# Joining triangular inverses: two heads per pass instead of one

## The chip, the cores and the metric

The kernel runs on one core of a Trainium2 chip. The time is device microseconds of one execution, the median of three runs. A core has TensorE (matrix products, written to PSUM), VectorE, ScalarE and GpSimd (work on tiles in SBUF and PSUM) and SyncE, which here only issues transfers. Each engine works off its own instructions in order; semaphores tie them together. Tiles lie over up to 128 partitions; a tile in PSUM takes a bank of its own here, and the kernel's pools hold eight of them. TensorE's array of 128 by 128 can be used in part: a product whose operands lie in partitions 32 to 63 uses one *row group*, and the partitions of its output pick the *column group*. Two products on different groups can be in the array together. All numbers here are float32, and each matrix product appears as two MATMUL instructions in the trace, each with its weight load.

## The reference

One block of a transformer: a gated delta-rule attention over 8 sequences of 256 tokens, with 16 key heads of width 128 and two value heads for each, and then a sparse feed-forward layer. What matters here is the recurrence:

```python
def step(S, inp):
    q_t, k_t, v_t, b_t, d_t = inp
    Sk = jnp.einsum('bhi,bhipj->bhpj', k_t, S)
    dv = b_t[..., None] * (v_t - Sk)
    upd = jnp.einsum('bhi,bhpj->bhipj', k_t, dv)
    S = S * d_t[:, :, None, :, None] + upd
    o = jnp.einsum('bhi,bhipj->bhpj', q_t, S)
    return (S, o)
...
x = x + ga * _L0_attn_ref(h, ...)
...
x = x + gb * _L0_ffn_ref(h, ...)
return x
```

The kernel does not step through the tokens. It cuts each sequence into two chunks of 128 tokens and solves a chunk at once: that takes the inverse T of a 128 by 128 triangular matrix (ones on the diagonal, and in the triangle the products of keys, weighted by decay and beta), for each sequence, chunk and value head.

## The kernel before

The work goes by *groups*: two sequences (`bp`) and four key heads (`GH = 4`), 16 groups in all. A *head* below is one key head for two sequences; it has 2 sequences x 2 chunks x 2 value heads = 8 triangular matrices (`NP = 8`, of which `NS = 4` belong to each sequence). There are 64 heads.

For each group, ahead of its use:

- `stage_a` (L479) makes the keys of a head (ps_k L432, then the convolution), their products ps_kk (L532) and the 8 triangles a_t (L563). It writes the four 32 by 32 diagonal blocks of each triangle to scr in DRAM.
- `stage_b` (L577) loads the blocks of all four heads (128 of them, one per partition) and inverts them by substitution on VectorE (L604, L610). It writes the inverses twice, to scr_y as they are and to scr_x transposed.

For each head then:

- `levels` (L674) joins the diagonal inverses to the full T in t_inv. For two neighbouring diagonal blocks with inverses X and Y, and the block A of the triangle between them, the block of T is -X A Y. It is done twice: 32-wide (blocks 0 with 1 and 2 with 3, both for 8 triangles), then 64-wide (upper with lower half). Each level is two bursts of matmuls with copies between them: ps_w L703 (A by X), copied to w1 (L711, L712); ps_t L717 (by Y), negated into t_inv (L729, L738), and, transposed on VectorE (L725, to `low`), into x_top (L732); ps_w2 L743/L746, copied to w2 (L750); ps_t2 L754/L757, negated into t_inv (L760, L761). In the trace ps_w2 and ps_t2 stand under the names ps_w and ps_t, as numbers are left out.
- In the 32-wide bursts the matmuls use two squares of the array in turn (`h` in 0, 1): rows 0 to 31 to columns 32 to 63, and rows 64 to 95 to columns 96 to 127 in ps_w, the other way round in ps_t. In the 64-wide bursts the first four triangles go from the upper 64 rows to the lower 64 columns, and the last four, whose operands are moved to the other half through low_up and x_top, from the lower rows to the upper columns.
- `prepare` (L619) makes queries, values and the gate of the next head (ps_qv L432, ps_z L646). `attend` (L764) uses T for one sequence of the head (ps_v L779, ps_kq L791 to L795, ps_u L810, ps_ks L818, ps_o L837 and L859, ps_u L853), `shares` projects two heads' outputs (ps_y L907).
- `feed_forward` (L160) of finished sequences and `ahead` (the next group's stage_a and stage_b) are pushed along a step at a time by `along` (L1089).

The loop over heads (L1102) is a round robin of generators: each turn asks attend of both sequences of this head, levels of the next head, and prepare of the next head for one step. Each head's levels thus run during the head before, the first head's of a group during the last head of the group before, after `all_of(background)` has finished stage_b (L1131). t_inv has two buffers, one in use by attend, one being made. The scheduler turns this trace into an order for each engine beforehand; the order of one engine does not change at run time.

Two more things matter. PSUM is shared by pools: ps_inv (L86, two banks) holds the bursts of levels, ps_kk, ps_ff (L183) and ps_out (L238); ps_in and ps_mix (three banks each) hold the rest. And SyncE issues all transfers of levels: two to x_even (L687), four to t_inv (L690), four to x_top (L693), and two to low_up (L697, L730) per head.

## Time and profile before

| what | value |
|---|---|
| median of three runs | 2133.49 us (2126.72 to 2134.71) |
| span of the profiled execution | 2126.1 us |
| mean granted TensorE clock | 0.988 |
| PE busy | 2054.1 us (97%) |
| DVE busy | 1660.8 us (78%) |
| ACT busy | 1356.1 us (64%) |
| POOL busy | 367.8 us (17%) |
| matmuls of levels: L703, L717 (32-wide) | 2048 instructions each, median 191 ns |
| matmuls of levels: L743, L746, L754, L757 (64-wide) | 512 instructions each, median 218 ns |
| copies of levels on ACT: L711, L712, L729, L738, L750, L760, L761 | 64 of each, 363 to 380 ns |
| the same, L732 | 128, 308 ns |
| transposes of levels on DVE: L725 | 64, median 430 ns |
| transfers of levels on SyncE, from issue to landing | 1.9 to 2.5 us (medians by line) |

The profile is one execution, and its time is its span (from the first to the last instruction). PE is TensorE, PEld its weight loads, DVE VectorE, ACT ScalarE, POOL GpSimd, SP SyncE. Matmuls overlap each other, so the duration of one is longer than the time from its start to the next start, and a busy TensorE is not one at its peak. In a line of the groups, "out<-in" names the tiles, then come the shapes and the count, the busy time and the mean of one, and the idle time just before with what ended it. In the timeline, a row is a run of like instructions: its start, how long it took, and the count.

### The profile page before, as it was taken

What the parts mean: (1) busy time and instruction counts of PE and PEld (TensorE: products, weight loads), DVE (VectorE), ACT (ScalarE), POOL (GpSimd) and SP (SyncE); (2) the same over time, 40 slices, a digit from 0 to 9 for tenths busy, and PEclk for the clock granted to TensorE, in tenths of its full rate; (3) what the DMA queues carried; (4) which work ended last, traced back from release to release, by engine and by line L of the source; (5) the groups of instructions that cost most, each with busy time, mean ns of one, the idle gap of its engine ahead of it and who ended that gap; (6) DMA issues with size and microseconds to landing.
All of it is one profiled execution on the core that took longest, in us unless ns stands there. A gap on an engine that the chain in (4) does not pass through costs nothing.

```text
span 2126.1 us, 46444 instructions
## 1 busy us (share of the span) xinstructions
PE 2054.1 (97%) x16684; PEld 1633.6 (77%) x16684; DVE 1660.8 (78%) x4039; ACT 1356.1 (64%) x4579; POOL 367.8 (17%) x375
## 2 busy tenths in 40 slices
PE   8989999999999999999999999999999999999998
PEld 5567777777777787778778687778778778787887
DVE  6788787878879587897878779787896958879357
ACT  3577767776766467576576666667666656666552
POOL 3121202112120111212021020211112011120010
PEclk9999999999999999999999999999999999999999
DMA  4342424233242443434343343443434244343236
GB/s 135 98 112 69 113 66 118 79 78 113 82 116 82 124 118 92 124 97 120 115 103 102 117 117 104 113 118 98 121 98 120 67 124 129 96 114 96 73 90 216
DMA packets 324517, 226.85 MB, mean 107 GB/s; under 512 B 254520, under 2 KB 266168, under 8 KB 324288
## 3 DMA queue, kind: packets, MB, share of 16 engines
q1 hardware_dynamic: 304416, 163.34, 28.8%
q10 hardware_dynamic: 19872, 60.54, 9.1%
q8 instruction: 133, 2.18, 0.4%
q14 instruction: 96, 0.79, 0.1%
HBM read 186.28 MB, written 29.12 MB: 101 GB/s over the span
## 4 chain that ended last, share of the span: by engine, by line
PE 66%; DVE 13%; DMA 7%; ACT 6%; issue 2%; SPq 1%; POOL 1%; ACTq 0%; DVEq 0%; POOLq 0%
PE ps_qv L432 10%; PE ps_y L907 9%; PE ps_z L646 8%; PE ps_ks L818 5%; PE ps_ff L190 4%; PE ps_k L432 3%; DVE cv L420 3%; PE ps_u L853 2%; PE ps_out L244 2%; PE ps_o L837 2%; PE ps_kk L532 2%; PE ps_gt L893 2%; PE ps_o L859 2%; DMA blk<-scr 2%; PE ps_u L810 2%
## 5 line engine op out<-in xcount | busy, mean ns | idle before, releaser
L420 DVE SCALAR_TENSOR_TENSOR cv<-ps_qv,conv_sb,cv 128x510 f32<-128x510 f32 (+1 forms) x564 | 410.0, 736 | 43.4 <-ACT cv L418 41.5
L432 PE MATMUL ps_qv<-h_bp,wh 128*128 128x512 f32 x768 | 367.3, 602 | 3.0 <-DVE cv L420 2.0
L105 POOL TENSOR_TENSOR rs<-ss,minus_halves 128x4 f32<-128x4 f32 x128 | 133.2, 1049 | 1040.8 <-DVE ss L864 1023.7
L646 PE MATMUL ps_z<-wh,h_bp 128*128 128x256 f32 x1024 | 249.9, 386 | 12.1 <-ACT gz L653 11.3
L907 PE MATMUL ps_y<-wo,og_p 128*128 128x256 f32 x1024 | 236.0, 380 | 0.9 <-DVE cv L420 0.9
L646 PEld LDWEIGHTS ps_z<-wh,h_bp 128*128 128x128 f32 x1024 | 186.3, 192 | 39.8 <-ACT gz L653 12.4
L432 PEld LDWEIGHTS ps_qv<-h_bp,wh 128*128 128x128 f32 x768 | 133.3, 192 | 105.4 <-issue 97.8
L418 ACT ACTIVATE cv<-ps_qv,conv_sb 128x512 f32<-128x512 f32 x188 | 129.3, 690 | 122.3 <-PE ps_qv L432 121.9
L907 PEld LDWEIGHTS ps_y<-wo,og_p 128*128 128x128 f32 x1024 | 188.0, 190 | 23.7 <-DVE cv L420 1.4
L604 DVE TENSOR_TENSOR tmp<-blk 128x30 f32<-128x30 f32 (+14 forms) x480 | 157.1, 327 | 46.8 <-DMA blk<-scr 37.6
L516 POOL TENSOR_TENSOR diag<-consts,bk 128x1032 f32<-128x1032 f32 x64 | 122.8, 1918 | 371.6 <-DVE bk L507 371.6
L844 ACT ACTIVATE junk<-o 128x128 f32<-128x128 f32 x512 | 154.1, 305 | 42.9 <-DVE o L860 36.4
L551 DVE TENSOR_TENSOR_SCAN e<-dbc,diag 128x1032 f32<-128x1032 f32 x60 | 137.9, 2299 | 47.6 <-POOL diag L516 46.3
L610 DVE TENSOR_TENSOR blk<-blk,tmp 128x30 f32<-128x30 f32 (+14 forms) x480 | 156.9, 327 | 9.6
L420 DVE SCALAR_TENSOR_TENSOR k_t<-ps_k,conv_sb,k_t 128x510 f32<-128x510 f32 (+1 forms) x189 | 139.2, 738 | 22.0 <-ACT k_t L418 20.3
L877 DVE SCALAR_TENSOR_TENSOR og<-o,rs,gz 128x128 f32<-128x128 f32 x512 | 143.9, 345 | 14.1 <-POOL rs L105 14.0
L818 PE MATMUL ps_ks<-u,cross 128*128 128x128 f32 x1024 | 144.7, 284 | 2.8 <-DVE aq L800 1.5
L784 ACT ACTIVATE vn<-ps_v,nk 128x256 f32<-128x256 f32 x256 | 105.7, 482 | 62.0 <-PE ps_v L779 61.2
L818 PEld LDWEIGHTS ps_ks<-u,cross 128*128 128x128 f32 x1024 | 133.7, 197 | 12.5 <-ACT u L812 5.3
L190 PE MATMUL ps_ff<-h,w_ff 128*128 128x128 f32 x1024 | 130.5, 277 | 3.3 <-ACT h L149 2.3
L190 PEld LDWEIGHTS ps_ff<-h,w_ff 128*128 128x128 f32 x1024 | 123.5, 192 | 10.8 <-issue 3.8
L432 PE MATMUL ps_k<-h_bp,wk 128*128 128x512 f32 x256 | 123.9, 609 | 2.0 <-ACT junk L451 1.2
(176 smaller groups left out, 4259.2 us busy)
## 6 DMA issues: line engine op xcount, KB each, us to landing
wh<-in_w_heads ACTq DMA_DIRECT2D x64, 640.0 KB, 4.1
w_ff<-in_w_ff SPq DMA_DIRECT2D x128, 256.0 KB, 3.0
dbc<-d_dram SPq DMA_DIRECT2D x60, 516.0 KB, 4.2
wo<-in_w_heads ACTq DMA_DIRECT2D x32, 512.0 KB, 3.7
w_dn<-in_w_down SPq DMA_DIRECT2D x64, 256.0 KB, 3.4
wk<-in_w_keys SPq DMA_DIRECT2D x16, 512.0 KB, 5.0
scr<-a_t SPq DMA_DIRECT2D x256, 32.0 KB, 2.4
blk<-scr SPq DMA_DIRECT2D x16, 512.0 KB, 3.7
```

Of the source, the lines that this page charges most:

```text
L105: nc.gpsimd.tensor_tensor(out=out, in0=in_, in1=minus_halves[:, :n], op=ALU.pow)
L190: nc.tensor.matmul(ps[:, a, l, :], lhsT=w[:, k, l, :], rhs=h2[:, k, :], start=(k == 0), stop=(k == CC - 1),)
L420: nc.vector.scalar_tensor_tensor(out=dst[:, :, d:], in0=ps[:, :, : T - d], scalar=taps[:, KC - 1 - d : KC - d], in1=dst[:, :, d:], op0=ALU ...
L432: nc.tensor.matmul(ps.rearrange("p b t -> p (b t)"), lhsT=w[k], rhs=h_bp[:, k, :], start=(k == 0), stop=(k == CC - 1),)
L551: nc.vector.tensor_tensor_scan(e.rearrange("p i s t -> p (i s t)"), dbc.rearrange("p i f -> p (i f)"), diag.rearrange("p s t -> p (s t)"), ...
L604: nc.vector.tensor_tensor(out=tmp, in0=blk[:, j, None, j + 1 :].to_broadcast([P, j, m]), in1=blk[:, 0:j, j, None].to_broadcast([P, j, m]), ...
L610: solved = nc.vector.tensor_tensor(out=blk[:, 0:j, j + 1 :], in0=blk[:, 0:j, j + 1 :], in1=tmp, op=ALU.subtract)
L646: nc.tensor.matmul(ps[:, n, :], lhsT=h_bp[:, k, i * T + n * P : i * T + (n + 1) * P], rhs=wh[:, k * 640 + 384 : (k + 1) * 640], start=(k = ...
L818: nc.tensor.matmul(ps_ks[:, ct, h, :], lhsT=cross[:, h, ct, :], rhs=u0[:, h, :], start=True, stop=True)
L844: nc.scalar.activation(junk, o[:, n, h, :], AF.Square, accum_out=ss[:, n, h : h + 1])
L877: nc.vector.scalar_tensor_tensor(out=og[:, n, h, :], in0=o[:, n, h, :], scalar=rs[:, 2 * n + h : 2 * n + h + 1], in1=gz[:, i, n, h, :], op ...
L907: nc.tensor.matmul(ps_y[:, n, :], lhsT=og_p[:, j // 2, i, n, j % 2, :], rhs=wo[:, j // 2, j % 2, :], start=(j == 0), stop=(j == 3),)
```

## The change

`levels` takes two heads at a time (`pair`, two records, and two t_inv buffers `tts`).

- The 32-wide bursts hold the matmuls of both heads: the first head's go from the even 32-row groups to the odd column groups in ps_w, the second head's from the odd row groups to the even column groups, and the other way round in ps_t. A new tile `moved` holds the second head's blocks on the partitions that this needs. All four write one PSUM bank, 64 instructions to a burst.
- One copy negates all of ps_w into w1; ps_t is copied unnegated in four pieces, and VectorE transposes its two lower pieces straight into x_top, so `low` goes.
- The 64-wide bursts hold the matmuls of both heads on all four 64 by 64 squares: the squares that write the same partitions write different banks, so each burst has two PSUM tiles (`i` = 0 for the first four triangles of a head, 1 for the last four), 32 instructions to a burst. w2 is copied with negation in two pieces, the result in four pieces without.
- Tiles grow: t_inv has three buffers instead of two, x_top, low_up and w2 double. The program is built with `dynamic_dma_scratch_size=1024`.
- The loop calls levels for heads 0 and 1 before the loop begins and for the next two heads in every second head (`hp` odd).

```diff
@@ -409,8 +409,8 @@
         modulation(0)
-        t_inv = [single.tile([P, 2 * NS, P], F32, name=f"t_inv{i}") for i in range(2)]
-        x_top = single.tile([P, NS, 2 * Q], F32, name="x_top")
+        t_inv = [single.tile([P, 2 * NS, P], F32, name=f"t_inv{i}") for i in range(3)]
+        x_top = single.tile([P, 2 * NS, 2 * Q], F32, name="x_top")
         for t in (*t_inv, x_top):
             nc.gpsimd.memset(t, 0.0)
@@ -671,94 +671,103 @@
                 step()
                 yield
-        def levels(rec, scr_x, scr_y, tt):
-            hp = rec["hp"]
+        def levels(pair, scr_x, scr_y, tts):
+            hp = pair[0]["hp"]
             xv = scr_x.rearrange("(g s q) a b -> g q a s b", g=GH, q=NQ)
             yv = scr_y.rearrange("(g s q) a b -> g q a s b", g=GH, q=NQ)
-            a_f = rec["a"].rearrange("p i s t -> p (i s) t")
+            a_f = [rec["a"].rearrange("p i s t -> p (i s) t") for rec in pair]
             NP = 2 * NS
+            def rows(q, n=1):
+                return slice(q * Q, (q + n) * Q)
             x_even = single.tile([P, NP, Q], F32, name="x_even")
-            low_up = single.tile([P, NS, 2 * Q], F32, name="low_up")
-            for q in (0, 2):
-                nc.sync.dma_start(out=x_even[q * Q : (q + 1) * Q], in_=xv[hp, q])
-            for q in (1, 3, 0, 2):
-                rows = slice(q * Q, (q + 1) * Q)
-                nc.sync.dma_start(out=tt[rows, :, rows], in_=yv[hp, q])
-                if q < 2:
-                    for i in range(2):
-                        nc.sync.dma_start(
-                            out=x_top[i * 2 * Q + q * Q : i * 2 * Q + (q + 1) * Q, :, rows],
-                            in_=xv[hp, q, :, i * NS : (i + 1) * NS],
-                        )
-            nc.sync.dma_start(out=low_up[2 * Q :], in_=a_f[0 : 2 * Q, NS:, 2 * Q :])
-            even = [slice(0, Q), slice(2 * Q, 3 * Q)]
-            odd = [slice(Q, 2 * Q), slice(3 * Q, P)]
+            moved = single.tile([P, NP, Q], F32, name="moved")
+            low_up = single.tile([P, NP, 2 * Q], F32, name="low_up")
+            for r in range(2):
+                for h in range(2):
+                    nc.sync.dma_start(out=x_even[rows(2 * h + r)], in_=xv[hp + r, 2 * h])
+            for h in range(2):
+                nc.sync.dma_start(out=moved[rows(2 * h + 1)], in_=a_f[1][rows(2 * h), :, rows(2 * h + 1)])
+            for q in (1, 3):
+                nc.sync.dma_start(out=tts[0][rows(q), :, rows(q)], in_=yv[hp, q])
+                nc.sync.dma_start(out=moved[rows(q - 1)], in_=yv[hp + 1, q])
+            for r in range(2):
+                for q in range(2):
+                    nc.sync.dma_start(out=x_top[rows(2 * r + q), :, rows(q)], in_=xv[hp + r, q])
+            for r, q in ((0, 2), (1, 2), (1, 3), (0, 0), (1, 0), (1, 1)):
+                nc.sync.dma_start(out=tts[r][rows(q), :, rows(q)], in_=yv[hp + r, q])
+            nc.sync.dma_start(out=low_up[rows(2, 2)], in_=a_f[1][rows(0, 2), :, rows(2, 2)])
             ps = bank(ps_inv, [P, NP, Q], "ps_w")
             for s in range(NP):
                 for h in range(2):
+                    even, odd = rows(2 * h), rows(2 * h + 1)
                     nc.tensor.matmul(
-                        ps[odd[h], s, :],
-                        lhsT=a_f[even[h], s, odd[h]],
-                        rhs=x_even[even[h], s, :],
-                        start=True,
-                        stop=True,
+                        ps[odd, s, :], lhsT=a_f[0][even, s, odd], rhs=x_even[even, s, :], start=True, stop=True
+                    )
+                    nc.tensor.matmul(
+                        ps[even, s, :], lhsT=moved[odd, s, :], rhs=x_even[odd, s, :], start=True, stop=True
                     )
             w1 = single.tile([P, NP, Q], F32, name="w1")
-            nc.scalar.copy(w1[odd[0]], ps[odd[0]])
-            nc.scalar.copy(w1[odd[1]], ps[odd[1]])
+            nc.scalar.activation(w1, ps, AF.Copy, scale=-1.0)
             yield
             ps = bank(ps_inv, [P, NP, Q], "ps_t")
             for s in range(NP):
                 for h in range(2):
+                    even, odd = rows(2 * h), rows(2 * h + 1)
                     nc.tensor.matmul(
-                        ps[even[h], s, :],
-                        lhsT=w1[odd[h], s, :],
-                        rhs=tt[odd[h], s, odd[h]],
-                        start=True,
-                        stop=True,
+                        ps[even, s, :], lhsT=w1[odd, s, :], rhs=tts[0][odd, s, odd], start=True, stop=True
                     )
-            low = mixp.tile([Q, NP, Q], F32, tag="low", name="low", bufs=1)
-            nc.vector.transpose(
-                low.rearrange("p s t -> p (s t)"),
-                ps[even[0]].rearrange("p s t -> p (s t)"),
-            )
-            nc.scalar.activation(tt[even[1], :, odd[1]], ps[even[1]], AF.Copy, scale=-1.0)
-            nc.sync.dma_start(out=low_up[0 : 2 * Q], in_=tt[2 * Q :, NS:, 2 * Q :])
+                    nc.tensor.matmul(
+                        ps[odd, s, :], lhsT=w1[even, s, :], rhs=moved[even, s, :], start=True, stop=True
+                    )
+            for r in range(2):
+                nc.scalar.copy(tts[r][rows(2), :, rows(3)], ps[rows(2 + r)])
             for i in range(2):
-                nc.scalar.activation(
-                    x_top[i * 2 * Q + Q : (i + 1) * 2 * Q, :, 0:Q],
-                    low[:, i * NS : (i + 1) * NS],
-                    AF.Copy,
-                    scale=-1.0,
-                )
-            nc.scalar.activation(tt[even[0], :, odd[0]], ps[even[0]], AF.Copy, scale=-1.0)
-            yield
-            top, bottom = slice(0, 2 * Q), slice(2 * Q, P)
-            ps = bank(ps_inv, [P, NS, 2 * Q], "ps_w2")
+                part = slice(i * NS, (i + 1) * NS)
+                nc.sync.dma_start(out=low_up[rows(0, 2), part], in_=tts[1 - i][rows(2, 2), part, rows(2, 2)])
+            for r in range(2):
+                nc.vector.transpose(x_top[rows(2 * r + 1), :, rows(0)], ps[rows(r)])
+            for r in range(2):
+                nc.scalar.copy(tts[r][rows(0), :, rows(1)], ps[rows(r)])
+            yield
+            halves_of = rows(0, 2), rows(2, 2)
+            top, bottom = halves_of
+            first, second = slice(0, NS), slice(NS, NP)
+            lhs = a_f[0][top, :, bottom], low_up[bottom]
+            ps = [bank(ps_inv, [P, NS, 2 * Q], f"ps_w2{i}") for i in range(2)]
             for s in range(NS):
-                nc.tensor.matmul(
-                    ps[bottom, s, :], lhsT=a_f[top, s, bottom], rhs=x_top[top, s, :], start=True, stop=True
-                )
-                nc.tensor.matmul(
-                    ps[top, s, :], lhsT=low_up[bottom, s, :], rhs=x_top[bottom, s, :], start=True, stop=True
-                )
-            w2 = single.tile([P, NS, 2 * Q], F32, name="w2")
-            nc.scalar.copy(w2, ps)
-            yield
-            ps = bank(ps_inv, [P, NS, 2 * Q], "ps_t2")
+                for i in range(2):
+                    for r in range(2):
+                        nc.tensor.matmul(
+                            ps[i][halves_of[r if i else 1 - r], s, :],
+                            lhsT=lhs[r][:, i * NS + s, :],
+                            rhs=x_top[halves_of[r], i * NS + s, :],
+                            start=True,
+                            stop=True,
+                        )
+            w2 = single.tile([P, NP, 2 * Q], F32, name="w2")
+            for i, part in enumerate((first, second)):
+                nc.scalar.activation(w2[:, part], ps[i], AF.Copy, scale=-1.0)
+            yield
+            ps = [bank(ps_inv, [P, NS, 2 * Q], f"ps_t2{i}") for i in range(2)]
             for s in range(NS):
-                nc.tensor.matmul(
-                    ps[top, s, :], lhsT=w2[bottom, s, :], rhs=tt[bottom, s, bottom], start=True, stop=True
-                )
-                nc.tensor.matmul(
-                    ps[bottom, s, :], lhsT=w2[top, s, :], rhs=low_up[top, s, :], start=True, stop=True
-                )
-            nc.scalar.activation(tt[top, 0:NS, bottom], ps[top], AF.Copy, scale=-1.0)
-            nc.scalar.activation(tt[top, NS:, bottom], ps[bottom], AF.Copy, scale=-1.0)
+                for i in range(2):
+                    for r in range(2):
+                        side = halves_of[r if i else 1 - r]
+                        p = i * NS + s
+                        nc.tensor.matmul(
+                            ps[i][halves_of[r], s, :],
+                            lhsT=w2[side, p, :],
+                            rhs=tts[r][bottom, p, bottom] if r == i else low_up[top, p, :],
+                            start=True,
+                            stop=True,
+                        )
+            for i, part in enumerate((first, second)):
+                for r in range(2):
+                    nc.scalar.copy(tts[r][top, part, bottom], ps[i][halves_of[r]])
             yield
         def attend(rec, i, cv, gz, eps_q, tt, og_t):
@@ -1075,7 +1084,6 @@
         waiting = iter(())
         units = []
         head = 0
-        solved = False
         for g, (bp, k0) in enumerate(groups):
             ya = y_of[bp % 2]
             next_recs, next_scratch = [], []
@@ -1106,8 +1114,8 @@
                     gen, shared = prepared[head]
                     with tc.issue_after(first_solved):
                         all_of(gen)
-                if not solved:
-                    for _ in levels(rec, *scratch, t_inv[head % 2]):
+                if head == 0:
+                    for _ in levels(recs[:2], *scratch, [t_inv[r] for r in range(2)]):
                         along()
                 turns, ends[:] = ends[:], []
                 if hp % 2 == 0:
@@ -1122,19 +1130,19 @@
                             ),
                         )
                     waiting = shares(ya, k0 + hp == 0, og_p, wo, 6)
-                turns += [attend(rec, i, *shared, t_inv[head % 2], og_p[:, hp % 2, i]) for i in range(2)]
-                solved, coming = False, None
+                turns += [attend(rec, i, *shared, t_inv[head % 3], og_p[:, hp % 2, i]) for i in range(2)]
+                coming = None
                 if hp + 1 < GH:
-                    coming = recs[hp + 1], scratch
+                    coming = recs[hp + 1 : hp + 3], scratch
                 elif g + 1 < len(groups):
                     all_of(background)
-                    coming = next_recs[0], next_scratch
+                    coming = next_recs[:2], next_scratch
                 if coming:
-                    solved = True
-                    turns.append(levels(coming[0], *coming[1], t_inv[(head + 1) % 2]))
+                    if hp % 2 == 1:
+                        turns.append(levels(coming[0], *coming[1], [t_inv[(head + r) % 3] for r in (1, 2)]))
                     if head > 0:
-                        to_come = coming[0]
+                        to_come = coming[0][0]
                         gen, shared = begin(to_come["kh"], to_come["bp"], to_come["h"])
                         turns.append(gen)
                 while turns:
@@ -1207,7 +1215,7 @@
         "w_down": w_down,
         "table": table,
     }
-    nc = bacc.Bacc("TRN2", target_bir_lowering=False, num_devices=1)
+    nc = bacc.Bacc("TRN2", target_bir_lowering=False, num_devices=1, dynamic_dma_scratch_size=1024)
     sent, args = {}, {}
     for name, a in arrays.items():
         a = np.ascontiguousarray(a)
```

## The prediction

> **What bounds the kernel now.** I read the page first, then the groups of instructions with shapes kept apart, then TensorE's timeline in one head (1012 to 1037 us) and across one change of group (1058 to 1092 us), then the waits by line.
>
> ```profile
> span 2126.1 us, 46444 instructions
> PE 2054.1 (97%) x16684; PEld 1633.6 (77%) x16684; DVE 1660.8 (78%) x4039; ACT 1356.1 (64%) x4579; POOL 367.8 (17%) x375
> ...
> PE   8989999999999999999999999999999999999998
> ...
> L703 PE MATMUL ps_w<-x_even,a_t 32*32 32x32 f32 x2048 | 53.7, 194 | 7.0 <-DMA x_even<-scr_x 6.9
> ...
> L743 PE MATMUL ps_w<-x_top,a_t 64*64 64x64 f32 x512 | 45.4, 230 | 3.8 <-ACT x_top L732 2.5 <-DMA out<-res 1.3
> ...
> 1013.00 0.69 PE L703 MATMUL ps_w<-x_even,a_t 32*32 32x32 f32 x32
> 1013.62 1.13 PE L432 MATMUL ps_qv<-h_bp,wh 128*128 128x512 f32 x2
> ...
> 1031.14 0.22 PE L743 MATMUL ps_w<-x_top,a_t 64*64 64x64 f32 x1
> 1031.14 0.22 PE L746 MATMUL ps_w<-x_top,low_up 64*64 64x64 f32 x1
> 1031.20 0.22 PE L743 MATMUL ps_w<-x_top,a_t 64*64 64x64 f32 x1
> 1031.20 0.22 PE L746 MATMUL ps_w<-x_top,low_up 64*64 64x64 f32 x1
> 1031.26 0.22 PE L743 MATMUL ps_w<-x_top,a_t 64*64 64x64 f32 x1
> ...
> 1047.56 1.88 PE L432 MATMUL ps_qv<-h_bp,wh 128*128 128x512 f32 x4
> 1049.28 0.59 PE L791 MATMUL ps_kq<-cv,k_t 128*128 128x256 f32 x2
> ...
> 47.96 1.85 PE L399 MATMUL ps_m<-sc_t,wmod_ss 128*128 128x8 f32 x16
> 49.73 0.60 PE L1049 MATMUL ps_gate<-wmod_gates,sc_t 128*8 128x512 f32 x1
> ...
> PEld ps_w L703 <- DMA x_even<-scr_x: 8.8, 10, 2.4
> ```
>
> TensorE is busy in every slice, but busy hides pipelining, so I go by starts. Four 512-column matmuls start 1.72 us before what follows (1047.56 to 1049.28): 430 ns each, where the "mean of one" says 602. Pricing every matmul by the spacing of its shape (512 columns 430 ns, 256 columns 216, 128 columns 111, and the joins below) gives 1908 us of work in the 2126.1. The other 200 us, **9.4%**, is waiting, some 30 of it the ends of the small bursts. So TensorE's issue sets the end nine tenths of the time; VectorE (78%) and ScalarE (64%) follow it. What shortens TensorE's queue shortens the span.
>
> The joins (L703, L717, L743/L746, L754/L757) run once per head, 64 times. A 32-wide burst has 32 instructions (16 matmuls, two instructions each) and holds the queue 0.62 us (1013.00 to 1013.62). Single starts inside it alternate 7 ns and 25 ns: the two row groups start almost together, and a step of two takes 32 ns. Entry and exit add 21 and 96 ns. In a 64-wide burst the pair again starts within 7 ns (both shown at 1031.14) and the next at 1031.20: 58 ns a step, median burst 0.612 us. Together 64 x 2 x (0.624 + 0.612) = 158 us, 7.4% of the span.
>
> What sets a step? With 8 moving columns, 16 matmuls still start 111 ns apart ((49.73 - 47.96) / 16): that is the load of 128 weight columns, as long as streaming 128. By halves, 58 and 32 ns are both the load and the stream of a 64- and a 32-wide square. A step is set within its squares, and issue (7 ns) has room for four.
>
> **32-wide joins on four squares.** The new order is odd-from-even of the first head and even-from-odd of the second: each square has a row group and a column group of its own, so the case is the present one with four instead of two. A step stays at 32 ns if four starts fit (4 x 7 = 28 ns, just). A burst for two heads: 0.624 + two more starts of 7 ns = 0.638 us. 128 x 0.624 = 79.9 becomes 64 x 0.638 = 40.8: **-39 us**. If four row groups gave nothing, a burst would have 32 steps: 0.624 + 16 x 0.032 = 1.13 us, saving only the ends, -7.
>
> All four row groups write one bank. The Trainium skill, "TensorEngine Tiling (Array Packing)", Gotcha 1: PSUM Pressure, says that different row tiles cannot use one PSUM bank at the same time, which speaks against this part. In the fence L743 and L746 use different row groups, write one tile ps_w in one bank, and start together at 58 ns a step, as one of them alone would need. By the rule this part would bring -7, by the row -39.
>
> **64-wide joins on all four squares.** Now two squares share each row group (with different columns) and two share each column group (in different banks). The trace has no such case. Lower bound, by the 58 ns step: 8 steps of four, 0.612 + 2 x 7 ns = 0.626 us per two heads; 128 x 0.612 = 78.3 becomes 40.1: -38. Middle, squares of one row group take turns: 16 half steps, 0.612 + 8 x 0.058 = 1.08 us, 69.1 in all: -9. Upper, they also cannot load weights while the other streams: (58 + 58) x 2 = 233 ns a step, 8 x 0.233 + 0.15 = 2.0 us, 129: +51. I take **-38**: the nearest row is the pair of squares that ignore each other.
>
> The Trainium skill, "TensorE: Matmul & The Clock Gate", Part 3, The mechanism, says that a weight load overlaps a running matmul only in another row group. That would put this part near the upper bound. But the weights of L743 are loaded while the previous L743 streams on the same rows, or its step would be 117 and not 58 ns; whether that holds for a neighbour square no run here shows yet.
>
> **ScalarE and VectorE.** Now per head: 363 + 364 (w1), 374 + 373 (t), 2 x 308 (x_top), 369 (w2), 376 + 380 ns: 3.2 us, 206 in all. After, per pair: one w1 copy 370, four of 374, two of 370, four of 378: 4.1 us, 132 in all, so 74 us less ScalarE work. It is not the bound; I take nothing. The transposes stay two of 431 ns per pair, now straight into x_top, but between the t copies: x_top is ready 0.75 + 0.86 = 1.6 us after the matmuls instead of 0.43 + 0.37 + 0.62 = 1.4. Bounds: waits in front of L717, L743 and L754 that ScalarE ends come to some 30 us, half could go (-15); 32 chains of 0.2 to 0.6 us more, all exposed, +18. I take 0. Covered by projections and by the other sequence's attention; without that cover, +18.
>
> **SyncE's queue.** 23 transfers per pair instead of 24. But the first burst needs four x_even, not two: 2 x 0.45 us later (SyncE's median issue is 448 ns). That counts where the joins wait for freshly solved blocks, at the 15 changes of group: x_even is what TensorE waits for there (0.57 us at 1071.8). Behind it queue ps_qv and ps_kq. Between 0 and 14 us; I take **+10**, as that wait is already exposed in most groups. The transfers behind (t_inv, x_top) are needed 9 us later. The third t_inv and the smaller scratch for dynamic transfers: nothing, the page's list of transfers has none issued by GpSimd, and t_inv's buffers are written a head ahead as before.
>
> **PSUM banks.** Pool ps_inv has two banks, shared with ps_ff, ps_out and ps_kk. Each 64-wide stage now takes both. Today a bank is held, by the trace's starts and copies, 1.45 us (ps_w2) and 2.06 us (ps_t2) on average; with one and two more copies 1.8 and 2.8, less the bursts: 3.4 us per pair in which feed-forward or k.k matmuls cannot begin. Nothing if other matmuls stand in the queue there, 32 x 3.4 = 109 us if nothing does. TensorE finds no work 9.4% of the time today: **+10**.
>
> **The sum.** -39 - 38 = -77. A tenth of it (9.4%) falls where TensorE was not what was waited for: +7. With +10 and +10: -50, so 2126.1 becomes 2076. The span is that of one profiled execution; the shortest of the three runs took 2126.72 and the median 2133.49, 7.4 more than the span. On the median's scale **2083 us**, -2.4%.
>
> **The rivals.** *Forecast*: both parts work. 57%, 2050 to 2105. For it: spacing, not busy time, follows the squares. *The 64-wide squares take turns by row group*: -39 - 9 + 26 = -22, 2112 us, 17%. For it: nothing in the trace shares a row group. Against: loads already overlap streams within one. *The two banks become the bound*: TensorE's queue is in order, so one ps_ff that waits for a bank holds everything behind it. All gains given back when 60 of the 109 us are exposed, 1.9 us per pair; with all of it 2133 - 77 + 109 + 17 = 2182 us. For it: the long holds, two banks for four users, and joins in every second head only, so their gaps and fillers no longer come evenly. Against: ps_qv, ps_z, ps_y and the attention use other pools. 12%. *Squares collide* (the upper bound): -39 + 51 + 27 = +39, 2172 us; decides from a step of about 0.17 us for four. 8%. *Gain and new waits cancel*: 6%, 2123 to 2144.
>
> **How the numbers follow.** A measurement of this kernel cannot tell less than 0.5% (11 us) from no change. Faster by more: 57 + 17 = 74%; within: 6%; slower: 12 + 8 = 20%. The range goes from all gains with ScalarE's 15 us and no costs for waits or banks beyond a few us (2133 - 77 - 4 = 2052) to 2126, past the second case; the forecast's own range is 2050 to 2105.
>
> **What would show it.** L703's successor: 64 instructions in about 0.64 us; 1.1 us would refute four row groups. The 64-wide burst of 32: 0.63 us (forecast), 1.08 (turns), 2.0 (collision). TensorE's waits before ps_ff, ps_kk, ps_out and the joins that end on ScalarE copies of the joins, above 60 us in sum, mean the bank rival. Waits on x_even should grow by some 10 us and ScalarE's busy time fall by 74. The prediction is wrong if the bursts shrink as said and the time does not.

## The result, and the profile after

The changed kernel takes 2268.56 us (median of 4 runs, 2263.89 to 2270.26) against 2130.1 us of the kernel before on the same chip: the ratio is 1.065, with an interval of 1.062 to 1.067. It was forecast at 2083 us and is 138 us slower than before instead of some 50 faster. (One profile below, that of e13, is of a disturbed execution and is not read; e15 repeats it.)

The page of the changed kernel: span, busy engines, and the shares of the chain that ended last; then the same shares of the kernel before.

```profile
span 2266.1 us, 46015 instructions
PE 2055.3 (91%) x16684; PEld 1632.2 (72%) x16684; DVE 1641.9 (72%) x4039; ACT 1290.0 (57%) x4358; POOL 372.0 (16%) x376
...
PE 31%; DVE 29%; DMA 11%; ACT 4%; issue 3%; SPq 2%; POOL 2%; DVEq 0%; POOLq 0%; ACTq 0%
```

```profile
PE 66%; DVE 13%; DMA 7%; ACT 6%; issue 2%; SPq 1%; POOL 1%; ACTq 0%; DVEq 0%; POOLq 0%
```

A wait of SyncE's queue, in the kernel before and in the changed one (who waits for what: us in all, times, the longest in us):

```profile
SPq L596 <- ACT xb L592: 248.0, 11, 32.2
SPq L596 <- ACT xb L592: 547.2, 15, 48.9
```

No engine has noticeably more to do: ScalarE is busy 66 us less, VectorE 19 us less. The chain, though, runs 29% through VectorE (13% before) and only 31% through TensorE (66% before). The waits say that the transfer of the finished substitution (L596) waits 547 us in all for its last copy (248 before). Priced as in the prediction, by the spacing of each shape, TensorE's work fell from 1908 to 1881 us, and its waits (time between starts beyond these prices, slower pace included) rose from 201 to 369.

The bursts themselves came out much as drawn. First a 32-wide burst of the changed kernel and its successor on TensorE, then a 64-wide one:

```profile
1144.25 0.21 PE L707 MATMUL ps_w<-x_even,a_t 32*32 32x32 f32 x1
1144.25 0.21 PE L710 MATMUL ps_w<-x_even,moved 32*32 32x32 f32 x1
...
1144.93 1.98 PE L432 MATMUL ps_k<-h_bp,wk 128*128 128x512 f32 x4
```

```profile
352.50 0.27 PE L744 MATMUL ps_w<-x_top,a_t 64*64 64x64 f32 x1
352.50 0.27 PE L744 MATMUL ps_w<-x_top,low_up 64*64 64x64 f32 x1
...
353.13 0.27 PE L744 MATMUL ps_w<-x_top,a_t 64*64 64x64 f32 x1
353.14 0.27 PE L744 MATMUL ps_w<-x_top,low_up 64*64 64x64 f32 x1
...
353.66 0.27 PE L761 MATMUL ps_t<-t_inv,w 64*64 64x64 f32 x1
```

64 instructions of two heads take 0.68 us (0.64 forecast). The 64-wide one takes 1.16 us, but not since the squares are in each other's way: the fixed order has 16 instructions for the one bank and then, 0.63 us later, 16 for the other, so only two squares run at a time. Where the order does mix the banks (in 6 of 64 stages), single starts come 7, 7, 6 and 39 ns apart, 59 ns for four. In the rows of such a stage, where the timeline merges neighbours into x2, the low_up squares come in twos at 270.63, 270.68 and 270.74, the t_inv squares likewise between them:

```profile
270.63 0.23 PE L761 MATMUL ps_t<-low_up,w 64*64 64x64 f32 x2
270.64 0.26 PE L761 MATMUL ps_t<-t_inv,w 64*64 64x64 f32 x2
270.68 0.23 PE L761 MATMUL ps_t<-low_up,w 64*64 64x64 f32 x2
270.70 0.26 PE L761 MATMUL ps_t<-t_inv,w 64*64 64x64 f32 x2
270.74 0.22 PE L761 MATMUL ps_t<-low_up,w 64*64 64x64 f32 x2
```

**Where the time went.** A group's cycle is a loop: the first head's ps_u (L810; L819 after), the next group's keys and triangles (to the end of a_t L563), the transfer to scr and back, the substitution (first L604 to last L610), and from its end the transfers and joins to the next ps_u. Means over 14 groups, in us; work is TensorE's by spacing and VectorE's busy time:

| stretch | before | TensorE, VectorE | after | TensorE, VectorE |
|---|---|---|---|---|
| ps_u to end of a_t | 49.4 | 45.0, 35.1 | 53.9 | 45.4, 35.3 |
| to the first L604 | 9.3 | 8.5, 5.2 | 8.3 | 8.0, 3.9 |
| substitution | 45.7 | 42.5, 43.3 | 51.1 | 48.3, 49.5 |
| to the next ps_u | 20.9 | 18.4, 16.4 | 21.5 | 11.1, 10.0 |
| group | 125.3 | 114.4, 100.0 | 134.8 | 112.8, 98.7 |

The same in the trace, for one group: the windows of the substitution and of the link behind it, before and then after. Columns are the stretch, its length, and the busy time and count of PE, PEld, DVE, ACT and POOL, the granted clock, and the DMA share and GB/s.

```profile
1528.40:1571.90 43.50, 40.79 (x245) 33.84 (x244) 40.68 (x115) 23.22 (x77) 4.01 (x6) 0.96 0.26 79
1571.90:1594.20 22.30, 22.05 (x216) 15.40 (x216) 19.15 (x36) 18.25 (x56) 5.17 (x5) 1.00 0.39 107
```

```profile
1628.30:1678.20 49.90, 49.26 (x266) 38.73 (x265) 48.80 (x135) 29.98 (x94) 4.96 (x7) 1.00 0.24 71
1678.20:1702.20 24.00, 16.37 (x246) 11.87 (x244) 13.74 (x26) 11.20 (x37) 4.25 (x4) 0.96 0.54 137
```

VectorE is busy through the first window in both kernels (40.68 of 43.50, 48.80 of 49.90). TensorE is too (40.79 and 49.26), so the rows alone do not say which of them bounds it. e5 below does: with fewer other instructions on VectorE the stretch falls to 39.5 us, VectorE is still busy 36.5 of them, and TensorE has only some 26 us of work. After, VectorE has 135 instructions there instead of 115, and the link has 26 instead of 36: work that used to fill the link is now done ahead of it. The link is a chain of latencies and does not get shorter; it gets empty. This is what TensorE does in it from 1684 on, the joins left out:

```profile
1684.58 3.72 PE L646 MATMUL ps_z<-wh,h_bp 128*128 128x256 f32 x16 [1.60 <-ACT junk L451]
...
1688.91 1.98 PE L432 MATMUL ps_k<-h_bp,wk 128*128 128x512 f32 x4
1690.73 0.60 PE L447 MATMUL ps_n2q<-consts,cv 128*128 128x128 f32 x4
1691.17 0.60 PE L447 MATMUL ps_n2k<-consts,k_t 128*128 128x128 f32 x4
...
1702.20 1.22 PE L819 MATMUL ps_u<-vn,t_inv 128*128 128x128 f32 x4
```

Between 1691.8 and 1702.2 there is little but the joins and their waits (and one ps_y of 1.1 us); the longest wait is the transfer low_up, 3.93 us in the chain. In the last 10 us of its link (1584.2 to 1594.2) the kernel before still had a ps_qv, the ps_z and a ps_k to do:

```profile
1584.27 1.88 PE L432 MATMUL ps_qv<-h_bp,wh 128*128 128x512 f32 x4
1585.99 1.89 PE L646 MATMUL ps_z<-wh,h_bp 128*128 128x256 f32 x8
...
1588.42 1.99 PE L646 MATMUL ps_z<-wh,h_bp 128*128 128x256 f32 x8
1590.25 1.88 PE L432 MATMUL ps_k<-h_bp,wk 128*128 128x512 f32 x4
```

The table has one thing more. Of the 9.5 us that a group loses, 5.4 stand in the substitution and 4.5 in the stretch from ps_u to the end of a_t, where TensorE has next to no more work (45.4 against 45.0). What fills that stretch was not taken apart. Some of it may be pace: the granted clock is at half for 6.0 us of it (1.9 before), and for 7.1 us of the emptied link (0.1 before), in the mean of the same groups.

### The profile page after: what moved, and what is told of

Its sections match the earlier page's. It is cut to its first block, busy times and chain, and to the rows that moved or that the text cites. A ratio compares the mean times of both kernels' runs of the same rounds, so it can differ in the third digit from the quotient of the medians.

```text
span 2266.1 us, 46015 instructions
## 1 busy us (share of the span) xinstructions
PE 2055.3 (91%) x16684; PEld 1632.2 (72%) x16684; DVE 1641.9 (72%) x4039; ACT 1290.0 (57%) x4358; POOL 372.0 (16%) x376
## 4 chain that ended last, share of the span: by engine, by line
PE 31%; DVE 29%; DMA 11%; ACT 4%; issue 3%; SPq 2%; POOL 2%; DVEq 0%; POOLq 0%; ACTq 0%
DVE cv L420 8%; PE ps_y L916 6%; PE ps_qv L432 3%; PE ps_ff L190 3%; DVE blk L610 3%; DVE tmp L604 3%; DVE k_t L420 2%; DVE og L886 2%; DVE e L551 2%; PE ps_z L646 2%; DMA blk<-scr 2%; PE ps_ks L827 2%; DMA low_up<-t_inv 2%; DMA x_even<-scr_x 2%; DVE aq L809 2%
## 5 line engine op out<-in xcount | busy, mean ns | idle before, releaser
L420 DVE SCALAR_TENSOR_TENSOR cv<-ps_qv,conv_sb,cv 128x510 f32<-128x510 f32 (+2 forms) x564 | 409.1, 738 | 21.3 <-ACT cv L418 19.3
L916 PE MATMUL ps_y<-wo,og_p 128*128 128x256 f32 x1024 | 247.6, 391 | 11.6 <-ACT t_inv L727 6.4
L604 DVE TENSOR_TENSOR tmp<-blk 128x30 f32<-128x30 f32 (+14 forms) x480 | 156.7, 326 | 46.2 <-DMA blk<-scr 38.5
L563 DVE TENSOR_TENSOR a_t<-ps_kk,e 128x512 f32<-128x512 f32 x128 | 82.0, 682 | 124.1 <-PE ps_kk L532 122.9
L610 DVE TENSOR_TENSOR blk<-blk,tmp 128x30 f32<-128x30 f32 (+14 forms) x480 | 156.3, 326 | 7.5
L841 ACT ACTIVATE o<-ps_ks,g_in 128x128 f32<-128x128 f32 x256 | 80.0, 364 | 86.0 <-DVE rr L832 75.8
```

What stands on the lines that cost most here:

```text
L420: nc.vector.scalar_tensor_tensor(out=dst[:, :, d:], in0=ps[:, :, : T - d], scalar=taps[:, KC - 1 - d : KC - d], in1=dst[:, :, d:], op0=ALU ...
L604: nc.vector.tensor_tensor(out=tmp, in0=blk[:, j, None, j + 1 :].to_broadcast([P, j, m]), in1=blk[:, 0:j, j, None].to_broadcast([P, j, m]), ...
L610: solved = nc.vector.tensor_tensor(out=blk[:, 0:j, j + 1 :], in0=blk[:, 0:j, j + 1 :], in1=tmp, op=ALU.subtract)
L916: nc.tensor.matmul(ps_y[:, n, :], lhsT=og_p[:, j // 2, i, n, j % 2, :], rhs=wo[:, j // 2, j % 2, :], start=(j == 0), stop=(j == 3),)
```

## The experiments

Theories, as they came: **A**, the pair's chain at the change of group is too long and uncovered; **B**, the two banks of ps_inv; **C**, the new tiles; **D**, the substitution is pushed back in VectorE's order; **A'**, the waits of the pair's own joins for transfers and copies, wherever the pair stands (the "rival" of the later runs); **F**, the 64-wide joins of a pair; **G**, D with its reason: in the third head of a group (head 2, counted from 0), where the substitution runs, there are no joins any more, TensorE and VectorE run ahead there and spend the cover of the link. `levels_one` below is `levels` of the kernel before, in the changed kernel's tiles. Each ratio is to the kernel before on the same chip.

**e1 to e4: where the pair stands, and the banks.** e1 puts `levels_one` for every head, e2 for heads 0 and 1 of a group, e3 for heads 2 and 3:

```diff
-                    if hp % 2 == 1:
+                    if hp == 1:                      # e2; e3: hp == 3
                         turns.append(levels(coming[0], ...))
+                    elif hp != 2:                    # e3: hp in (1, 2)
+                        turns.append(levels_one(coming[0][0], *coming[1], t_inv[(head + 1) % 3]))
```

e4 is the changed kernel with other pools:

```diff
-    ps_in = ctx.enter_context(tc.tile_pool(name="ps_in", bufs=3, space=PSUM))
-    ps_inv = ctx.enter_context(tc.tile_pool(name="ps_inv", bufs=2, space=PSUM))
+    ps_in = ctx.enter_context(tc.tile_pool(name="ps_in", bufs=2, space=PSUM))
+    ps_inv = ctx.enter_context(tc.tile_pool(name="ps_inv", bufs=3, space=PSUM))
```

> All joins one head at a time as before, but with the changed kernel's tiles (three t_inv, wide x_top, low_up, w2) and its smaller scratch. If the loss lies in pairing (theories A and B), this is the kernel before again: 2115 to 2150 us. If the new tiles or the scratch cost (theory C): above 2200.

Measured: 2118.73 us, ratio 0.996 (0.993 to 0.998). The new tiles and the scratch cost nothing; C falls.

> Heads 0 and 1 of each group joined one at a time, heads 2 and 3 as a pair, away from the change of group. Theory A (the loss is a chain of joins for two heads right behind the substitution at the change of group, with too little queued beside it): no loss left, 2090 to 2145 us. Theory B (a pair's 64-wide stage takes both banks of ps_inv, wherever it stands): half of the loss stays, 2180 to 2220.

Measured: 2259.13 us, ratio 1.062 (1.056 to 1.067): nearly the whole loss, though the change of group has its old short chain.

> The mirror of the last: heads 0 and 1 of each group joined as a pair at the change of group, heads 2 and 3 one at a time. Theory A: most of the loss, 2200 to 2280 us. Theory B: the same half as in the mirror case, 2180 to 2220, and equal to it.

Measured: 2157.75 us, ratio 1.014 (1.009 to 1.019). A and B both fall: the place that A blamed costs 1.4%, the harmless one 6%, and B wanted them equal.

> The changed kernel with three banks for ps_inv and two instead of three for ps_in. Theory B: most of the loss goes, 2100 to 2170 us, and the 64-wide bursts come as one of 32 instructions. Theory A: little changes, 2240 to 2300, and the waits for x_even, x_top and low_up stay.

Measured: 2294.0 us, ratio 1.078 (1.073 to 1.084). A third bank does not help; as ps_in lost one, this alone settles nothing (the loss stands elsewhere here: 60.3 us from ps_u to the end of a_t, 43.3 for the substitution). The banks are settled by e13.

In the trace of e2 a substitution takes 51.4 us, VectorE is busy 49.7 of them, and TensorE has 11.9 us of work in the 21.5 us of the link: the figures of the changed kernel. In e3 they are 45.7, 43.5 and 18.6 of 23.4: those of the kernel before, with a link 2.5 us longer. What e2 shares with the changed kernel and e3 does not is that head 3 is joined together with head 2, so that no joins are left in the third head.

**e5 to e8: the order.** e5 and e6 (the kernel before) put what a turn gives VectorE behind the substitution step that stands before it:

```diff
-                    with tc.issue_after(first_solved) if head == 0 else ExitStack():
+                    with tc.issue_after(first_solved if head == 0 else last[0]):
```

e7 keeps the 32-wide part of the change and does the 64-wide joins of the two heads one after the other, in one bank each:

```diff
-            ps = [bank(ps_inv, [P, NS, 2 * Q], f"ps_w2{i}") for i in range(2)]
+            for r in range(2):
+                ps = bank(ps_inv, [P, NS, 2 * Q], f"ps_w2{r}")
...
```

e8 spreads the next group's work over fewer turns:

```diff
-                while done < work * rounds / (total * 3 / 4):
+                while done < work * rounds / (total * 11 / 16):
```

> The changed kernel, with one more rule for the fixed order: what a turn of the heads' loop gives VectorE comes behind the substitution step that stands before it in the program. In VectorE's order that leaves 50 other instructions among the 60 of a substitution, against 79 in the changed kernel and 62 in the one before. Theory D (the substitution, the link between two groups, was pushed back in VectorE's order once the second head's joins left the third head): the stretch of a substitution falls from 51 to about 45 us and the time to 2140 to 2200. Theory A' (the waits of the pair's own joins for transfers and copies are the loss): 2240 to 2290.

Measured: 2241.45 us, ratio 1.054 (1.052 to 1.055).

> The same rule in the kernel before (45 other instructions instead of 62 among the substitution's). Control: theory D says that the substitution hardly bounds there, 2090 to 2150 us; whatever this gains is not owed to the pairing.

Measured: 2238.28 us, ratio 1.052 (1.050 to 1.055).

The stretch fell further than expected, to 39.5 us in e5 and 38.7 in e6, and yet the time did not: the rule holds back the running heads' own work as well, and the link grows to 28.1 us in both. So a short substitution by itself is worth nothing; D as it stood falls. e5's time lies in the range of A', but e6, which has no pair, is as slow. What the two show: under one and the same order rule the kernels differ by 3 us and no longer by 138. That points to the order and not to the joins, but does not prove it: both are some 110 us slower than the kernel before, and the long link may hide what the joins cost.

> The changed kernel with its 32-wide joins on pairs, but the 64-wide joins one head at a time as before (one bank each), both heads still in the same place. Theory D: the third head has no joins here either and 81 other instructions stand among the substitution's, so the loss stays, 2230 to 2290 us. Theory F (the 64-wide joins of a pair, with both banks and their low_up waits, are the loss): 2110 to 2160.

Measured: 2274.32 us, ratio 1.070 (1.068 to 1.072). F falls: a pair whose 64-wide stages come head by head, in one bank each, loses as much. On the banks it says less than its edit, since the changed kernel already ran one bank after the other in 58 of 64 stages.

> The changed kernel with the work for the next group spread over 22 of 32 turns instead of 24. Theory D: the substitution is ready some 5 us earlier in each of 15 groups (74 other instructions among it), 2170 to 2230 us. Theories A' and F: as the changed kernel, 2245 to 2290, since the joins' own waits stay.

Measured: 2243.22 us, ratio 1.054 (1.052 to 1.057): 25 us less than the changed kernel, a third of what D expected, and 2 us below the range of A' and F. The end of a_t comes 3.6 us earlier in a group, the substitution still takes 50.3.

**e9 to e12: hold the cover back, or add joins.** In e9, e10 (the kernel before) and e12 (the kernel of e3), only the preparation of the next group's first head is held:

```diff
+                held = turns[-1] if hp + 1 == GH and coming else None
+                def ask(t):
+                    with tc.issue_after(last[0]) if t is held else ExitStack():
+                        return next(t, turns) is not turns
...
-                        turns = [t for t in turns if next(t, turns) is not turns]
+                        turns = [t for t in turns if ask(t)]
```

e11 is e2 with `else:` for `elif hp != 2:`.

> The changed kernel; VectorE's part of the preparation of the next group's first head (convolution of queries and values) is put behind the last substitution step, all else is as changed. Theory G (the work that used to cover the 21 us from the end of a substitution to the next group's first ps_u is done too early, inside the stretch of the substitution, which VectorE bounds): the stretch falls from 51 to 43 to 47 us, TensorE has 15 us of work or more in the last 21 to 23 instead of 11, and the time is 2120 to 2200 us. Rival (the pair's own waits and longer chain make the loss, wherever the cover stands): 2230 to 2290.

Measured: 2233.35 us, ratio 1.050 (1.046 to 1.053).

> The same edit in the kernel before, as its control (53 other instructions among a substitution's instead of 62). Theory G: there the cover stands late already (18 of 21 us), so no more than 2090 to 2150 us; what it gains is not owed to the pairing.

Measured: 2192.81 us, ratio 1.031 (1.028 to 1.034).

G misses both, and e9's time lies in the rival's range. The edit costs the kernel before 3%, so it is no neutral control: TensorE's work in the link rises to some 19 us in both, as G said, but the link itself to 29 us (e9) and 27 (e10), and the way to a_t by 3 and 6. Between the two kernels the gap is 40 us here.

> The kernel of the run with the pair away from the change of group (2259 us), with work added: in the third head of each group the fourth head's joins are made once more, into the same buffer with the same values. That puts joins back where the kernel before had them, some 2.5 us of TensorE and 3 us of ScalarE per group more. Theory G (without these joins TensorE and VectorE run ahead in the third head and push the substitution back): faster in spite of more work, 2130 to 2210 us (68 others among a substitution's instead of 79). Rival (the pair's own waits): 2259 plus 16 times 2 us or so, 2260 to 2310.

Measured: 2211.71 us, ratio 1.040 (1.037 to 1.043). Some 2.5 us of TensorE's work are added to each group, and the time falls by 47 us: G's sign, a little above its range, and against the rival, which wanted it to rise.

> The kernel with the pair at the change of group (2158 us) and the edit that puts the next group's first preparation behind the substitution. If the remaining loss there (1.4%) is lost cover too: 2090 to 2135 us. If it is the pair's longer chain of transfers (four x_even, both low_up) and the feed-forward's wait: 2140 to 2180.

Measured: 2193.82 us, ratio 1.032 (1.028 to 1.034), outside both ranges. The edit by itself costs the kernel before 66 us (e10), so this run says nothing on the 1.4% of e3.

**e13 and e14: the two tests of G.** e13 moves the pair of e2 by one head; e14 is the changed kernel with the fourth head's joins done again in the third:

```diff
# e13, against e2
-                    if hp == 1:
+                    if hp == 0:
...
-                    elif hp != 2:
+                    elif hp != 1:
# e14, against the changed kernel
+                    elif hp == 2:
+                        turns.append(levels_one(coming[0][0], *coming[1], t_inv[(head + 1) % 3]))
```

> Heads 1 and 2 of each group joined as a pair in head 0, heads 0 and 3 one at a time (at the change of group and in head 2). So the stretch of the substitution keeps its joins and the change of group its short chain. Theory G: no loss is left and the pair's saving in TensorE's queue shows, 2085 to 2130 us, with a substitution of about 46 us. Rival (a pair away from the change of group costs 6% wherever it stands, by its own waits): 2180 to 2260.

Measured: 2126.61 us, ratio 1.000 (0.999 to 1.002).

> The changed kernel with both pairs, and the fourth head's joins made once more in the third head, into the same buffer. Theory G: faster than the changed kernel in spite of more work, 2180 to 2250 us. Rival: slower, 2280 to 2320.

Measured: 2197.64 us, ratio 1.034 (1.031 to 1.037).

Both tell for G and against the pair's own waits and its two banks: e13's pair takes both banks like the others. One pair per group, not at the change of group, costs 132 us when it empties the third head (e2) and nothing when it empties the second (e13). And redundant joins in the third head make the changed kernel 71 us faster (65 by the two ratios). The same two windows of e14, for the group that was shown above:

```profile
1576.50:1621.70 45.20, 44.28 (x296) 36.16 (x295) 43.06 (x121) 27.37 (x87) 2.67 (x4) 1.00 0.28 84
1621.70:1645.50 23.80, 23.58 (x281) 16.10 (x279) 20.55 (x38) 17.76 (x54) 5.15 (x5) 1.00 0.53 130
```

VectorE is back at 121 instructions in the substitution, and the link of 23.8 us is full again. Means over 14 groups: 45.4 us for the substitution, 18.3 us of TensorE's work in the link of 23.3. Yet e14 is still 3.4% slower than the kernel before: the link is 2.4 us longer, as in e3, and the way from ps_u to the end of a_t is 52.3 us instead of 49.4. Part of that is the added work; the rest is open.

**e15 and e16: why the harmless pair gains nothing.** e15 is e13 again; e16 is e13 with the `levels` of e7.

> The kernel with heads 1 and 2 as a pair once more, for an undisturbed profile: 2120 to 2130 us. Theory G: a substitution of 45 to 47 us and 17 us or more of TensorE's work in the 21 us behind it, as in the kernel before; the pair's bursts are shorter, and the time saved shows as waits of TensorE in other heads.

Measured: 2130.1 us, ratio 1.000 (0.998 to 1.002).

> Heads 1 and 2 as a pair in the 32-wide joins alone, the 64-wide joins one head at a time. If the pair's 64-wide stage with its two banks eats the gain: 2100 to 2118 us. If TensorE's queue is no longer what bounds the group: 2118 to 2140.

Measured: 2138.99 us, ratio 1.004 (1.002 to 1.006). The 64-wide stage on two banks does not eat the gain.

In e15 the substitution takes 45.8 us, with 17.2 us of TensorE's work in the link of 20.3, as expected. TensorE's work is 1895 us (14 less than before), its waits 220 us (19 more). The way from ps_u to the end of a_t has grown from 49.4 to 51.8 us with 46.0 us of work in it. What TensorE waits for there was not taken apart by a run.

## Why the prediction was wrong

- **The step that failed** is the reading "TensorE's issue sets the end nine tenths of the time", with "What shortens TensorE's queue shortens the span" and the term for it in the sum, "A tenth of it (9.4%) falls where TensorE was not what was waited for: +7". A busy TensorE, taken over the whole span, was read as the bound. But in the 45.7 us of each substitution VectorE is busy 95% and, as e5 shows, sets its length, and the 20.9 us behind it are a chain of latencies; TensorE was busy in both since the order happened to give it work there. Taking joins out of the third head moved that work. Instead of +7 us it cost some 108: the changed kernel's 138 less the 30 of e3, whose pair stands at the change of group alone (e2 puts the part at 132, so the two do not just add). Not all of that is the moved work alone: adding joins back regains 71 us in e14 and 47 in e11, and the 4.5 us from ps_u to the end of a_t stay unexplained. (The term had a slip besides: 1908 from 2126.1 leaves 218 us, not 200, some 11 of them before the first start of a matmul and behind the last. At 10.3% the term would be +8.)
- **What had to be counted and was not**: for an engine that is 97% busy, which loop through other engines is as long. The windows of before show two engines alike with no new run; it took e5 to tell which of them sets the stretch. The Trainium skill, "Perfetto Trace Analysis", Optimization Strategy, says that the most-contended engine may change over a kernel's regimes; here the windows of one group agree in part: in the first VectorE and TensorE are busy alike (94%), in the next TensorE 99% and VectorE 86%.
- **32-wide**: right for a whole burst, 0.68 us for 64 instructions against 0.638. But only 13 of the 32 ps_w bursts stay whole, and the priced work on these lines fell by some 25 us (27 in all less the 2 of the next item) instead of 39. Starts in the first half of a burst are 7, 6, 7 and 12 ns apart, 32 ns for four; in the second half they come in twos, 17 ns apart. Four row groups write one bank, which the Trainium skill, "TensorEngine Tiling (Array Packing)", Gotcha 1: PSUM Pressure, excludes; the measurement decides.
- **64-wide**: the squares behave as taken (59 ns for four), so "take turns" and "collide" were wrong rivals. But the order put the two banks one after the other in 58 of 64 stages, and TensorE's work on these lines fell by 2 us instead of 38. Of the -77 some 27 came.
- **ScalarE** -74: measured -66. **x_even** +10: TensorE's matmuls waited for it 6.9 us before and 31.9 after, 25 more. The four x_even alone are not the reason: in e3, whose pair at the change of group needs them too, that wait is 3.7 us.
- **Banks** +10, and as a rival 12%: the prediction's own sign for it, more than 60 us of TensorE's waits that end on ScalarE's copies of the joins, did not come (8.2 us in all, 6.4 of them before ps_y; 5.1 before the change), and e13's pair with both banks costs nothing. **The rival that was missing** is the one that came true: the order spends the cover of the substitution's link early.

## What to carry to other kernels

Work saved on the busiest engine is worth its time only if no loop through another engine is as tight; cut the steady state into its stretches and look at each engine's share in each before pricing anything. In a fixed order, removing work from a place also moves what stands around it: a burst that seems to be mere load can be what keeps the cover of a later latency in its place, and the test for that is to add redundant work back (e14: more work, 71 us less). Of the versions run, the best is the kernel before with the new tiles and three t_inv buffers, joins one head at a time (e1): 0.4% faster (0.2 to 0.7%).

## What the runs showed of the hardware

Four 64 by 64 squares, two of them on the same rows, load weights and stream at the same time: 59 ns for four, as for one pair. The trace before, which has 64-wide squares in twos only, could not show it.

TensorE's bursts run at half pace where the granted clock is at half. The clock's records in these traces know 1.0 and 0.5 alone. In the changed kernel 1280.3 to 1287.0 us is a stretch at 0.50: in it one pair starts 107 ns behind the other instead of 58, already before the wait of 1.43 us for low_up that ends at 1282.27, so it is not that wait that slows them. In all the changed kernel spends 208 us at half clock and the kernel before 50 (0.954 and 0.988 in the mean), most of the difference in the emptied link and the 20 us behind it. How much of the loss this makes no run shows.

```profile
1280.11 0.22 PE L744 MATMUL ps_w<-x_top,a_t 64*64 64x64 f32 x1
...
1280.17 0.22 PE L744 MATMUL ps_w<-x_top,a_t 64*64 64x64 f32 x1
...
1280.40 0.31 PE L744 MATMUL ps_w<-x_top,a_t 64*64 64x64 f32 x1
...
1280.51 0.31 PE L744 MATMUL ps_w<-x_top,a_t 64*64 64x64 f32 x1
...
1282.27 0.36 PE L761 MATMUL ps_t<-low_up,w 64*64 64x64 f32 x1 [1.43 <-DMA low_up<-t_inv]
...
1282.54 0.31 PE L761 MATMUL ps_t<-low_up,w 64*64 64x64 f32 x1
...
1282.64 0.31 PE L761 MATMUL ps_t<-low_up,w 64*64 64x64 f32 x1
```
